# Last shared expert of a Perceiver layer: order of VectorE's sums, place of the routed answers, a GpSimd drain and the output in quarters

## The chip, the core and the metric

The kernel runs on one core of a Trainium2 chip. The metric is the device time of one execution in microseconds, the median of several runs. Three runs of the kernel before gave 1395.56, 1396.55 and 1399.64 us. All data is float32.

## What is computed

512 tokens (8 batches of 64, 512 wide) pass through three residual blocks. The first is cross-attention to 8 x 1601 context rows, with a rational weight in place of the exponential; the second is causal self-attention; the third, in which the change lies, is a mixture of experts:

```python
sh     = gelu(xf @ sW1 + sb1)             # two shared experts, every token
shared = mean over the two of (sh @ sW2 + sb2)
gates  = xf @ rW + rb                     # eight routed experts
probs  = softmax(top_k(gates, 2))         # two of them for each token
moe    = sum_j probs[:, j] * (gelu(xf @ W1[e_j] + b1[e_j]) @ W2[e_j] + b2[e_j])
x      = x + shared + moe
```

## The kernel before, in words

**Stages.** Attention fills the span to about 980 us and plays no part here. The expert stage then runs blocks one after the other in `run` (L1324): shared expert 0's last token tile, the first half of shared expert 1 (`Halves`, hidden quarters 0 and 1), eight routed experts (`Routed`, the fullest first, with gathered rows), and the second half of shared expert 1 (`Halves`, quarters 2 and 3, `store=True`). After that stands a loop (L1418) for tokens beyond the experts' room, whose trip count is read from a tensor; every engine reads the count and takes the branch.

**The token sum** `res` [128, 4, 512] lies in SBUF throughout: four token tiles (`tt`) of 128 rows. Everything is added to it in place, and at the end it is written to `out`.

**Halves.** Its matrix products are done in seven block products instead of eight (`ORDER`, L322). Each unit n adds one block product into a PSUM bank; three banks are used, A by units 0, 2, 4 and 6, C by unit 1, and B by units 3 and 5. Since a bank goes on collecting after it was read, a later unit of the same bank must wait until the earlier value has been read. There are three sections:

- `hidden(q)` (L1162) makes one hidden quarter in seven units of four matmuls. Units 0, 2 and 3 are copied from PSUM by ScalarE (L1191). Units 1, 4 and 5 are "joined" by VectorE, which adds PSUM to the copy (L1175), and then ScalarE applies gelu in two instructions (L1169). Unit 6 gets gelu straight from PSUM.
- `combine` (L1199) makes the four sums t1 to t4 (`RIGHT`) of each finished hidden quarter, which the seven products of the second layer need as operands. Each is a VectorE instruction with two SBUF inputs (L1210).
- `rows` (L1212) makes the second layer in seven units of eight matmuls (both quarters). VectorE adds each to `res` (L1231), halved, since two shared experts are averaged. Unit 2 is the first that reads a sum (t2).

**Routed answers.** Each routed expert writes its rows to `ys_d` in device memory. Two units into the last block (`at[NEXP + 2, 1]`), `combine(ys_d, from_i)` (L1378) runs on GpSimd: for every tile and each of the two picks an indirect DMA gathers the rows (L1383), a GpSimd instruction multiplies them by the probability (L1387), and another adds them to `res` (L1388). There are eight of each, and the buffers come from the pool `sd`, which has five.

**What sets the order.** The loops give instructions in program order, and a scheduler in the tile framework orders each engine's instructions by priority. In the program it made, VectorE's queue in the last block reads: three joins of quarter 2, its four sums, three joins of quarter 3, its four sums, then seven additions to `res`. PE, ScalarE and VectorE take their instructions strictly in this order. SP issues nearly all DMAs, also the four of the output (`rows_out`, L1103): tiles 2 and 3 after unit 5, tiles 0 and 1 after unit 6. GpSimd issues its own DMAs, the gathers among them. When the loop's branch is not taken, all engines meet in a closing barrier (L1486), in which each engine first executes a DRAIN.

Of the kernel before, what the change touches and what calls it, by code (L numbers as in the profile page):

```python
# [14 lines left out]
ALU = mybir.AluOpType  # L15
# [7 lines left out]
NTT = NT // P  # L23
# [5 lines left out]
NEXP, NSH = 8, 2  # L29
# [46 lines left out]
def perceiver_kernel(  # L76
# [7 lines left out]
    nc = tc.nc  # L84
# [22 lines left out]
    def w8(name):  # L107
        return w8p.tile([P, NC, 512], F32, tag="w8", name=name)

    def at4(name):  # L110
        return atp.tile([P, 1024], F32, tag="at", name=name)

    def np2(name):
        return npp.tile([P, 512], F32, tag="np", name=name)

    def sd(name):
        return sdp.tile([P, 512], F32, tag="sd", name=name)

    def psa(name):
        return ps_a.tile([P, 512], F32, tag="a", name=name)  # L120
# [49 lines left out]
    res = big.tile([P, NTT, E], F32, name="res")  # L170
# [31 lines left out]
    for j in range(2):  # L202
        m = mask[j * SQ : (j + 1) * SQ, 0, :]
        nc.gpsimd.affine_select(
            out=m, in_=m, compare_op=ALU.is_ge, fill=NEG, base=0,
# [10 lines left out]
        out=tri, in_=ones, compare_op=ALU.is_gt, fill=0.0, base=0,  # L216
# [12 lines left out]
    ys_d = dram.tile([TOT + 1, E], F32, name="ys_d")  # L229
# [76 lines left out]
    def right_parts(x):  # L306
        return {"b11": x[:, 0:2, 0:HF], "b12": x[:, 0:2, HF:SEC],
                "b21": x[:, 2:4, 0:HF], "b22": x[:, 2:4, HF:SEC]}

    RIGHT = (("t1", "b12", "b11"), ("t2", "b22", "t1"), ("t3", "b22", "b12"), ("t4", "b21", "t2"))  # L310
    tparts = {}

    def context_part(i, k):
        if k == 0:
# [7 lines left out]
    ORDER = (("A", "a11", "b11"), ("C", "a12", "b21"), ("A", "s2", "t2"), ("B", "s1", "t1"),  # L322
             ("A", "s3", "t3"), ("B", "s4", "b22"), ("A", "a22", "t4"))

    def multiply(ps, w, x, keys, first=True, last=True):

        for k in range(2):
            for c in range(2):
                l, r = (w, x) if keys else (x, w)

                nc.tensor.matmul(  # L331
                    ps[:, k, :], l[:, c, k * P : (k + 1) * P], r[:, c, :],
                    start=first and k == 0 and c == 0, stop=last and c == 1,
                    skip_group_check=True,
                )
# [78 lines left out]
    for c in range(NC):  # L414
        nc.gpsimd.dma_start(
            out=odd_x[:, c, :],
            in_=ctxT[:, c * P : (c + 1) * P, SKV - 1 : SKV].rearrange("b p s -> p (b s)"),
# [424 lines left out]
    for i, (b, k) in enumerate(secs):  # L842
        if i == 0:
            plan.add(4 * FULL, first_keys)
            there[i] = plan.now
            for t in range(SPT):
# [4 lines left out]
                if t == 1:  # L851
                    for g in range(NG):
                        plan.add(FULL, lambda g=g: q_unit(g))
                    asked = plan.now
# [54 lines left out]
    for tt in range(NTT):  # L909
        gap = 5.0 if tt < NTT - 1 else 3.2  # L910
        for bb in range(2):
            b = 2 * tt + bb
# [32 lines left out]
    pr = gp.tile([P, NTT, 2], F32, name="pr")  # L945
# [4 lines left out]
    from_i = gp.tile([P, 2, NTT], I32, name="from_i")  # L950
# [150 lines left out]
    outT = out.rearrange("(tt p) e -> tt p e", p=P)  # L1101

    def rows_out(tt):  # L1103
        nc.sync.dma_start(out=outT[tt], in_=res[:, tt, :])
# [38 lines left out]
    class Halves:  # L1143
# [18 lines left out]
        def hidden(self, q):  # L1162

            st = {}

            def gelu(f, r, src=None):
                for k in range(2):
                    hc = q * QC + 2 * f + k
                    nc.scalar.activation(  # L1169
                        st[f, r][:, k], (st[f, r] if src is None else src)[:, k], AF.Gelu,  # L1170
                        bias=b1_t[:, self.e, hc : hc + 1],
                    )

            def join(f, r, ps):
                nc.vector.tensor_tensor(st[f, r], ps, st[f, r], ALU.add)  # L1175
                gelu(f, r)

            def unit(n):
                bank, a, b = ORDER[n]
                if n == 0:  # L1180
                    self.h[q] = w8("hq")
                    for f in range(2):
                        for r in range(2):
                            st[f, r] = self.h[q][:, 2 * f : 2 * f + 2, r * HF : (r + 1) * HF]
                fresh = bank not in st
                if fresh:
                    st[bank] = psa("ps_hh").rearrange("p (k n) -> p k n", k=2)
                ps = st[bank]
                multiply(ps, self.w[0, q][a], self.x[b], True, first=fresh)
                if n in (0, 2, 3):  # L1190
                    nc.scalar.copy(st[{0: (0, 0), 2: (0, 1), 3: (1, 1)}[n]], ps)  # L1191
                elif n == 6:
                    gelu(1, 0, ps)
                else:
                    join(*{1: (0, 0), 4: (1, 1), 5: (0, 1)}[n], ps)

            return [lambda n=n: unit(n) for n in range(len(ORDER))]

        def combine(self):  # L1199

            k = len(self.right)
            for q in self.qs:
                p = self.right[q] = right_parts(self.h[q])
                t = at4("ht").rearrange("p (k c s) -> p k c s", k=2, c=2)
                if not k:
                    self.t4 = at4("ht").rearrange("p (k c s) -> p k c s", k=2, c=2)
                p |= {"t1": t[:, 0], "t2": t[:, 1], "t3": p["b12"], "t4": self.t4[:, k]}
                k += 1
                for d, a, b in RIGHT:
                    nc.vector.tensor_tensor(p[d], p[a], p[b], ALU.subtract)  # L1210

        def rows(self):  # L1212

            st = {}

            def unit(n):
                bank, a, b = ORDER[n]
                fresh = bank not in st
                if fresh:
                    st[bank] = psa("ps_hr").rearrange("p (k n) -> p k n", k=2)  # L1220
                ps = st[bank]
                if n == 0:
                    self.combine()
                for q in self.qs:
                    multiply(
                        ps, self.w[1, q][a], self.right[q][b], False,
                        first=fresh and q == self.qs[0], last=q == self.qs[-1],
                    )
                f, r = ((0, 0), (0, 0), (0, 1), (1, 1), (1, 1), (0, 1), (1, 0))[n]
                y = res[:, 2 * r : 2 * r + 2, f * 256 : (f + 1) * 256]  # L1230
                nc.vector.scalar_tensor_tensor(y, ps, 1.0 / NSH, y, ALU.mult, ALU.add)  # L1231
                if self.store and n >= 5:
                    for tt in ((2, 3), (0, 1))[n - 5]:
                        rows_out(tt)

            return [lambda n=n: unit(n) for n in range(len(ORDER))]

# [137 lines left out]
            skip_runtime_bounds_check_because="an index that max_index gave among eight",  # L1375
        )

    def combine(src, idx):  # L1378

        for tt in range(NTT):  # L1380
            for j in range(2):
                g = sd("g")
                nc.gpsimd.indirect_dma_start(  # L1383
                    out=g, out_offset=None, in_=src[:, :],
                    in_offset=bass.IndirectOffsetOnAxis(ap=idx[:, j, tt : tt + 1], axis=0),
                )
                nc.gpsimd.tensor_scalar_mul(g, g, pr[:, tt, j : j + 1])  # L1387
                nc.gpsimd.tensor_add(res[:, tt, :], res[:, tt, :], g)  # L1388

    tops = []  # L1390

    def routing():
        for tt in range(NTT - 1):
# [10 lines left out]
            (0, 3): routing,  # L1404
            (2, 2): lambda: probabilities(tops.pop()),
            (2, 6): add_biases,
            (NEXP + 2, 1): lambda: combine(ys_d, from_i),
        },
    )

# [7 lines left out]
    with tc.For_i(0, n_over) as j:  # L1418
        run([Routed(expert_in(ovx_i, j), TOT + j * P, P, yo_d, 0)])

        m = gp.tile([P, 2, NTT], F32, name="m_in")
        nc.vector.tensor_single_scalar(m, left, 0.0, op=ALU.is_ge)
        ix = gp.tile([P, 2, NTT], F32, name="ix")
        nc.vector.tensor_single_scalar(ix, left, float(P), op=ALU.is_lt)
        nc.vector.tensor_mul(m, m, ix)
        nc.vector.scalar_tensor_tensor(ix, left, float(-P), m, ALU.add, ALU.mult)
        nc.vector.tensor_scalar_add(ix, ix, float(P))
        ix_i = gp.tile([P, 2, NTT], I32, name="ix_i")
        nc.vector.tensor_copy(ix_i, ix)
        nc.vector.tensor_scalar_add(left, left, float(-P))  # L1430
        combine(yo_d, ix_i)
        for tt in range(NTT):
            rows_out(tt)
# [56 lines left out]
```

## Time and profile before

| what | value |
|---|---|
| median of three runs | 1396.55 us |
| the profiled execution's own time | 1398.13 us |
| its span, first to last instruction | 1396.3 us |
| outside the span | 1.8 us |
| mean granted TensorE clock | 0.995 |
| busy: PE, VectorE (DVE), ScalarE (ACT), GpSimd (POOL) | 1364.5, 890.0, 642.7, 770.7 us |
| last block: first matmul of its hidden part | 1330.9 us |
| second layer (`ps_hr`): first matmul | 1360.6 us |
| last addition to `res` begins | 1384.95 us |

How to read it. A line of the timeline has the start in us, the length in us (of merged instructions, the whole stretch), the engine, the line of the kernel, the operation, what it writes and reads with sizes, and how many were merged. The bracket says how long the engine was idle before and whose end released it. "PE" are matmuls and "PEld" weight loads; a float32 matmul makes two records. A q behind an engine's name (SPq, POOLq) marks its instruction queue, with instructions that only wait, branch, drain or issue. The table of windows gives busy times in chosen stretches and the granted TensorE clock (PEclk, 1.00 is full).

### The profile page before, as it was taken

To read this page: it belongs to the slowest core of one execution; us is meant where nothing else is said; L and a number is where in the kernel's file an instruction comes from. 1 tells how busy PE (TensorE), PEld (TensorE's weight loads), DVE (VectorE), ACT (ScalarE), POOL (GpSimd) and SP (SyncE) were. 2 spreads that over 40 slices of the span, in tenths; PEclk is the share of its full clock that TensorE was granted. 3 is DMA by queue.
4 is the path that set the end of the run, shared out by engine and by line. 5 is a ranking of instruction groups with operands and counts; after the bars stand their busy time and mean duration, and the time that the engine had idled before them with its cause. 6 is when DMAs were issued, how large, how long until landed. Compare 5 with 4: busy or idle time off the path is not lost.

```text
span 1396.3 us, 36461 instructions
## 1 busy us (share of the span) xinstructions
PE 1364.5 (98%) x16080; PEld 1075.3 (77%) x16080; DVE 890.0 (64%) x646; ACT 642.7 (46%) x1339; POOL 770.7 (55%) x688
## 2 busy tenths in 40 slices
PE   8999999999999999999999999999999999999996
PEld 3678788787788787788878777555786799977775
DVE  4698999988899997889989988614420000000332
ACT  3556666566666666566656666322311111112230
POOL 6388899886789986878887877500200000000063
PEclk9999999999999999999999999999999999999998
DMA  7002112112400121111121115354555346789621
GB/s 228 31 3 70 32 33 77 62 33 70 160 32 32 47 92 40 32 64 39 47 92 33 62 49 187 97 191 159 193 208 199 126 176 239 280 319 325 219 61 38
DMA packets 84227, 156.34 MB, mean 112 GB/s; under 512 B 13306, under 2 KB 13338, under 8 KB 84068
## 3 DMA queue, kind: packets, MB, share of 16 engines
q1 hardware_dynamic: 77732, 136.94, 28.5%
q0 software_dynamic: 4704, 13.91, 2.9%
q10 hardware_dynamic: 1632, 3.15, 0.7%
q8 instruction: 127, 2.08, 0.6%
q14 instruction: 32, 0.26, 0.1%
HBM read 143.24 MB, written 10.72 MB: 110 GB/s over the span
## 4 chain that ended last, share of the span: by engine, by line
PE 86%; DVE 4%; ACT 4%; POOL 2%; issue 2%; DMA 0%; DVEq 0%; POOLq 0%
PE ps_k L331 17%; PE ps_v L331 16%; PE ps_h L1351 11%; PE y L1296 6%; PE ps_s L520 4%; PE y L1305 4%; PE ps_hr L331 3%; PE ps_o L570 3%; PE ps_h L817 3%; PE y L829 3%; PE ps_hh L331 3%; DVE neg L538 3%; PE ps_v L399 1%; PE ps_k L389 1%; ACT neg L535 1%
## 5 line engine op out<-in xcount | busy, mean ns | idle before, releaser
L538 DVE RECIPROCAL neg<-neg 128x512 f32<-128x512 f32 (+1 forms) x224 | 683.8, 3092 | 58.4 <-ACT neg L537 55.2
L539 POOL TENSOR_TENSOR at<-at,neg 128x512 f32<-128x512 f32 (+1 forms) x224 | 266.6, 1196 | 126.7 <-DVE neg L538 122.7
L551 POOL TENSOR_TENSOR tot<-tot,at 128x512 f32<-128x512 f32 (+1 forms) x176 | 223.9, 1272 | 12.8
L1351 PEld LDWEIGHTS ps_h<-xgT,w1t 128*128 128x128 f32 x1024 | 147.9, 191 | 38.5 <-issue 32.7
L1356 ACT ACTIVATE hT<-ps_h,b1e 128x128 f32<-128x128 f32 (+4 forms) x128 | 50.3, 393 | 261.0 <-PE ps_h L1351 235.0
L1287 POOL DMA_DIRECT2D ys_d<-yo x12 | 6.6, 549 | 287.2 <-DVE yo L1286 287.2
L537 ACT ACTIVATE neg<-neg,one_t 128x512 f32<-128x512 f32 (+1 forms) x224 | 162.2, 726 | 0.0
L1351 PE MATMUL ps_h<-xgT,w1t 128*128 128x128 f32 (+4 forms) x1024 | 161.0, 301 | 0.0
L535 ACT ACTIVATE neg<-ps_s 128x512 f32<-128x512 f32 (+1 forms) x224 | 130.2, 583 | 63.2 <-PE ps_s L520 51.8
L331 PE MATMUL ps_k<-tx,sk 128*128 128x256 f32 x552 | 129.8, 386 | 3.8 <-ACT kT L348 3.7
L536 ACT ACTIVATE at<-ps_s 128x512 f32<-128x512 f32 (+1 forms) x224 | 131.7, 591 | 0.0
L331 PE MATMUL ps_v<-sv,tx 128*128 128x256 f32 x552 | 129.0, 384 | 1.0 <-ACT v L344 1.0
L331 PEld LDWEIGHTS ps_k<-tx,sk 128*128 128x128 f32 x552 | 101.5, 190 | 23.5 <-ACT kT L348 4.5
L331 PEld LDWEIGHTS ps_v<-sv,tx 128*128 128x128 f32 x552 | 102.4, 190 | 17.2 <-ACT v L344 1.4
L1278 DVE COPY xgT<-pt_x 128x512 f32<-128x512 f32 (+3 forms) x12 | 6.8, 592 | 142.7 <-PE pt_x L1277 142.7
L1296 PE MATMUL y<-w2t,hT 128*128 128x512 f32 x192 | 96.1, 595 | 0.0
L344 ACT COPY v<-ps_v 128x512 f32<-128x512 f32 x92 | 56.0, 609 | 75.0 <-PE ps_v L331 75.0
L348 ACT ACTIVATE kT<-ps_k,bk_t 128x256 f32<-128x256 f32 x138 | 59.6, 499 | 60.0 <-PE ps_k L331 60.0
L331 PE MATMUL ps_k<-cx,wk 128*128 128x256 f32 x368 | 86.9, 385 | 0.0
L331 PE MATMUL ps_v<-wv,cx 128*128 128x256 f32 x368 | 86.1, 383 | 0.0
L520 PEld LDWEIGHTS ps_s<-qT,kT 32*64 32x64 f32 x6144 | 70.1, 130 | 18.6 <-issue 17.2
L331 PEld LDWEIGHTS ps_k<-cx,wk 128*128 128x128 f32 x368 | 68.1, 190 | 12.9 <-issue 2.3
(264 smaller groups left out, 2042.2 us busy)
## 6 DMA issues: line engine op xcount, KB each, us to landing
w1t<-in_W_dram SPq DMA_DIRECT2D x32, 1024.0 KB, 11.6
w2t<-in_W_dram SPq DMA_DIRECT2D x32, 1024.0 KB, 12.2
cx<-in_ctxT_dram SPq DMA_DIRECT2D x23, 1024.0 KB, 5.8
w1t<-in_sW_dram SPq DMA_DIRECT2D x12, 1024.0 KB, 5.1
w2t<-in_sW_dram SPq DMA_DIRECT2D x12, 1024.0 KB, 5.4
wo<-in_woT_dram SPq DMA_DIRECT2D x4, 1024.0 KB, 5.3
awq<-in_aWq_dram SPq DMA_DIRECT2D x4, 1024.0 KB, 5.2
awp<-in_aWp_dram SPq DMA_DIRECT2D x4, 1024.0 KB, 5.4
```

The source lines that it names most:

```text
L331: nc.tensor.matmul(ps[:, k, :], l[:, c, k * P : (k + 1) * P], r[:, c, :], start=first and k == 0 and c == 0, stop=last and c == 1, skip_gr ...
L344: nc.scalar.copy(dst, src)
L348: nc.scalar.activation(dst[:, k], src[:, k], AF.Identity, bias=bk_t[:, g : g + 1])
L520: nc.tensor.matmul(ps[j][h, k, g, :], kT[rows, g, h], qT[rows, g, b * SQ : (b + 1) * SQ], start=True, stop=True, skip_group_check=True,)
L535: nc.scalar.activation(neg, ps, AF.Relu, scale=-1.0)
L536: nc.scalar.activation(pos, ps, AF.Relu)
L537: nc.scalar.activation(neg, neg, AF.Identity, bias=one_t[:w])
L538: nc.vector.reciprocal(neg, neg)
L539: nc.gpsimd.tensor_add(pos, pos, neg)
L551: nc.gpsimd.tensor_add(tot, tot, at[:, :, i])
L1296: nc.tensor.matmul(self.y[k], hT[:, s : s + w], w2t, start=first, stop=last)
L1351: nc.tensor.matmul(ph[:, : blk.n], w1t[:, c, f : f + P], blk.x[:, c, :], start=c == 0, stop=c == NC - 1,)
```

## The change

- **Sums behind joins.** `combine` makes the sums of both quarters together, tied behind the last join (`issue_after(self.joined.ins)`), t1 and t2 of both first, then t3 and t4. VectorE's queue in both `Halves` blocks is now: six joins, eight sums, then the additions.
- **VectorE joins the routed answers.** GpSimd's multiply and add are dropped. After each of the additions of units 0 to 3 in the last block, VectorE executes two `scalar_tensor_tensor` on 128x512 (gathered rows times probability plus `res`, all from SBUF): the two answers of one tile.
- **GpSimd only gathers, and is drained.** All eight gathers are issued together, into buffers that come alternately from the pools `np` and `sd`. A `drain` on GpSimd stands directly behind the eighth.
- **Rows leave in quarters by two queues.** After units 3, 4, 5 and 6 a quarter of `res` (two tiles, 256 columns) is written, one tile by SP, one by ScalarE's queue: four DMAs of 128 KB on each in place of four of 256 KB on SP. The last unit's addition is made as two instructions of 128x256, one for each tile.

The overflow loop uses the same gather and join, and keeps whole-tile writes.

```diff
@@ Halves.hidden
             def join(f, r, ps):
-                nc.vector.tensor_tensor(st[f, r], ps, st[f, r], ALU.add)
+                self.joined = nc.vector.tensor_tensor(st[f, r], ps, st[f, r], ALU.add)
                 gelu(f, r)
@@ Halves.combine
-            for q in self.qs:
+            for k, q in enumerate(self.qs):
                 p = self.right[q] = right_parts(self.h[q])
...
-                for d, a, b in RIGHT:
-                    nc.vector.tensor_tensor(p[d], p[a], p[b], ALU.subtract)
+            with tc.issue_after(self.joined.ins):
+                for part in (RIGHT[:2], RIGHT[2:]):
+                    for q in self.qs:
+                        p = self.right[q]
+                        for d, a, b in part:
+                            nc.vector.tensor_tensor(p[d], p[a], p[b], ALU.subtract)
@@ Halves.rows
-                nc.vector.scalar_tensor_tensor(y, ps, 1.0 / NSH, y, ALU.mult, ALU.add)
-                if self.store and n >= 5:
-                    for tt in ((2, 3), (0, 1))[n - 5]:
-                        rows_out(tt)
+                for k in ((0, 1) if self.store and n == len(ORDER) - 1 else (slice(0, 2),)):
+                    added = nc.vector.scalar_tensor_tensor(
+                        y[:, k], ps[:, k], 1.0 / NSH, y[:, k], ALU.mult, ALU.add
+                    )
+                if not self.store:
+                    return
+                if n < NTT:
+                    with tc.issue_after(added.ins):
+                        for j in range(2):
+                            join_answer(back.pop((n, j)), n, j)
+                for f, r, at_n in ((0, 0, 3), (1, 1, 4), (0, 1, 5), (1, 0, 6)):
+                    if n == at_n:
+                        for k, queue in enumerate((nc.sync, nc.scalar)):
+                            tt = 2 * r + k
+                            fs = slice(f * 256, (f + 1) * 256)
+                            queue.dma_start(out=outT[tt, :, fs], in_=res[:, tt, fs])
@@ the routed answers
-                g = sd("g")
-                nc.gpsimd.indirect_dma_start(
...
-                nc.gpsimd.tensor_scalar_mul(g, g, pr[:, tt, j : j + 1])
-                nc.gpsimd.tensor_add(res[:, tt, :], res[:, tt, :], g)
+    def gather(src, idx, tt, j):
+        g = sd("g") if j else np2("g")
+        asked = nc.gpsimd.indirect_dma_start(
...
+        return g, asked
+    def join_answer(g, tt, j):
+        nc.vector.scalar_tensor_tensor(
+            res[:, tt, :], g, pr[:, tt, j : j + 1], res[:, tt, :], ALU.mult, ALU.add
+        )
+    def gather_all():
+        for tt in range(NTT):
+            for j in range(2):
+                back[tt, j], asked = gather(ys_d, from_i, tt, j)
+        with tc.issue_after(asked.ins):
+            nc.gpsimd.drain()
...
-            (NEXP + 2, 1): lambda: combine(ys_d, from_i),
+            (NEXP + 2, 1): gather_all,
```

More of the change, by code (lines that the diff above doesn't have):

```diff
@@ L1199, in combine @@
         def combine(self):
-            k = len(self.right)
-            for q in self.qs:
+            self.t4 = at4("ht").rearrange("p (k c s) -> p k c s", k=2, c=2)
+            for k, q in enumerate(self.qs):
                 p = self.right[q] = right_parts(self.h[q])
                 t = at4("ht").rearrange("p (k c s) -> p k c s", k=2, c=2)
-                if not k:
-                    self.t4 = at4("ht").rearrange("p (k c s) -> p k c s", k=2, c=2)
                 p |= {"t1": t[:, 0], "t2": t[:, 1], "t3": p["b12"], "t4": self.t4[:, k]}
-                k += 1
-                for d, a, b in RIGHT:
-                    nc.vector.tensor_tensor(p[d], p[a], p[b], ALU.subtract)
+            with tc.issue_after(self.joined.ins):
[4 more added lines that the diff above has]
+                            nc.vector.tensor_tensor(p[d], p[a], p[b], ALU.subtract)
         def rows(self):
@@ L1376, in expert_in @@
         )
+    def gather(src, idx, tt, j):
+        g = sd("g") if j else np2("g")
+        asked = nc.gpsimd.indirect_dma_start(
+            out=g, out_offset=None, in_=src[:, :],
+            in_offset=bass.IndirectOffsetOnAxis(ap=idx[:, j, tt : tt + 1], axis=0),
+        )
[3 more added lines that the diff above has]
+            res[:, tt, :], g, pr[:, tt, j : j + 1], res[:, tt, :], ALU.mult, ALU.add
+        )
+    back = {}
+    def gather_all():
[4 more added lines that the diff above has]
+            nc.gpsimd.drain()
     def combine(src, idx):
@@ L1381, in combine @@
             for j in range(2):
-                g = sd("g")
-                nc.gpsimd.indirect_dma_start(
-                    out=g, out_offset=None, in_=src[:, :],
-                    in_offset=bass.IndirectOffsetOnAxis(ap=idx[:, j, tt : tt + 1], axis=0),
-                )
-                nc.gpsimd.tensor_scalar_mul(g, g, pr[:, tt, j : j + 1])
-                nc.gpsimd.tensor_add(res[:, tt, :], res[:, tt, :], g)
+                join_answer(gather(src, idx, tt, j)[0], tt, j)
     tops = []
```

## The prediction

> **What bounds the kernel now.** First the chain of work that ended last: by engine it is matmul, and each part of the change must be a gap in it or its end.
>
> ```profile
> PE 86%; DVE 4%; ACT 4%; POOL 2%; issue 2%; DMA 0%; DVEq 0%; POOLq 0%
> ```
>
> Then PE's timeline of the last block, for a matmul that waited:
>
> ```profile
> 1347.31 3.62 PE L331 MATMUL ps_hh<-xt,sw 128*128 128x256 f32 x16
> 1353.61 2.82 PE L331 MATMUL ps_hh<-xt,sw 128*128 128x256 f32 x8 [2.68 <-ACT hq L1191]
> 1356.22 2.79 PE L331 MATMUL ps_hh<-xnT,sw 128*128 128x256 f32 x8
> 1358.85 1.89 PE L331 MATMUL ps_hh<-xt,w1t 128*128 128x256 f32 x8
> ```
>
> This is PE's only wait on another engine in the last block. Unit 4 of the last hidden quarter adds into the bank that ScalarE must first have copied for unit 2. After the wait eight records take 2.8 us, where they take 1.89. ScalarE and VectorE tell why:
>
> ```profile
> 1352.18 0.91 ACT L1169 ACTIVATE hq<-hq,b_t 128x256 f32<-128x256 f32 x2 [5.81 <-DVE hq L1175]
> 1352.99 1.05 ACT L1191 COPY hq<-ps_hh 128x512 f32<-128x512 f32 x2
> ...
> 1343.99 0.97 DVE L1210 TENSOR_TENSOR ht<-hq 128x512 f32<-128x512 f32 x1 [0.97 <-ACT hq L1169]
> 1345.00 3.19 DVE L1210 TENSOR_TENSOR ht<-hq,ht 128x512 f32<-128x512 f32 x1
> 1348.11 1.76 DVE L1210 TENSOR_TENSOR hq<-hq 128x512 f32<-128x512 f32 x1
> 1349.79 1.75 DVE L1210 TENSOR_TENSOR ht<-hq,ht 128x512 f32<-128x512 f32 x1
> 1351.46 0.68 DVE L1175 TENSOR_TENSOR hq<-ps_hh,hq 128x512 f32<-128x512 f32 x1
> ```
>
> The copy stands on ScalarE behind a gelu that waits 5.81 us for the join, and the join stands on VectorE behind four sums, which take 7.67 us where four of 0.69 would take 2.8. At the same time GpSimd executes multiplies and adds (from 1342.80 to 1354.20).
>
> Windows give the clock, and the list of the closing line gives the end:
>
> ```profile
> 1350.90:1353.60 2.70, 0.03 (x1) 0.00 (x0) 1.24 (x2) 1.42 (x4) 2.70 (x3) 1.00 0.00 0
> 1353.60:1358.00 4.40, 4.39 (x13) 3.58 (x14) 0.69 (x1) 1.18 (x3) 3.90 (x4) 0.62 0.22 60
> ...
> L1486 POOLq DRAIN  x3: 46/109/5140, 1390.3 to 1396.0; - x3
> L1486 SPq DRAIN  x3: 7/7/7, 1391.0 to 1395.7; - x3
> ...
> L1104 SPq DMA_DIRECT2D out_dram<-res x4: 332/370/1486, 1382.3 to 1386.1; - x4
> ```
>
> PE stands still and then gets a clock of 0.62. At the end GpSimd's first closing DRAIN takes 5.14 us from 1390.3, though its last add ended at 1372.2; the next takes 0.11.
>
> **1. Sums behind the joins.** In order of VectorE's queue the join of unit 1 no longer has sums ahead of it. In the three other hidden quarters, where no stretched sums stood ahead, PE never waited. At full clock sixteen records start every 3.45 us (1343.86 to 1347.31), so unit 4 would have started at 1350.76, not 1353.61: 2.85 us. The sixteen records from 1353.61 to 1358.85 took 5.24 in place of 3.45: 1.79. Together 4.6 us of PE, all on the path. The Trainium skill (TensorE: Matmul & The Clock Gate, section What's actually happening) has the half clock follow an idle window of about 3.4 us; by it a wait of 2.85 should cost nothing more, and this part would be worth 2.9. The row shows 0.62 right behind this wait and 1.00 two windows later, so I take 4.6. Ends: 2.9 and 4.7.
>
> What is late next? Eight sums now lie behind the last join, in both Halves blocks. Undisturbed they take 8 x 0.69 = 5.5 us. The last join ends 0.8 us before the second layer starts (1359.74 against 1360.58), so they end 4.7 after its start. Behind them stands the addition of unit 0, whose bank unit 2 needs 6.9 us after the start (two units of 3.45): with 0.69 the addition ends at 5.4, 1.5 us to spare. t2 of both quarters is ready by about 3.3. In the first Halves block the same holds (join ends 1017.55, rows start 1018.38), and no PE wait was there to win: nothing. GpSimd issues three DMAs there from 1018.55 to 1020.25 beside two-input sums, which stay at 0.69.
>
> **2. Answers on VectorE, gathers alone on GpSimd.** Removed: eight GpSimd multiplies of 1.59 and eight adds of 1.28, none on the chain. Added: eight VectorE instructions of 128x512. None is in the trace from SBUF with two inputs and a multiply; the nearest row is the addition at L1231, 0.69; even as long as the worst sum's mean here (7.67/4 = 1.92) they would sum to 15.4. I take 8 x 0.69 = 5.5. With sums, answers and additions VectorE works 5.5 + 5.5 + 4.8 = 15.8 us beside 24.2 us of PE: hidden. If the cover went, at most 1.5 us at the first bank. Behind a waiting answer would stand the additions that free PE's banks. The gathers were issued at 1337.91 and every 1.31 after, landing after 3.7 (median); their buffers are free (the new pool's were read by matmuls that end by 1333.7). Eight so end at 1337.91 + 8 x 1.31 + 3.7 = 1352.1; the first answer is due about 5.4 after the second layer's new start (1360.6 - 4.6 = 1356.0), 1361.4. No wait: nothing.
>
> **3. The drain.** In the changed program's order it stands directly behind the eighth gather, so 1348.4 to about 1353.5, with nothing behind it on GpSimd but reading the loop count, needed 20 us later. What it costs there lies beside PE; a loss is excluded for that reason. What it saves is open between 0 (the price is that of the closing, or of the 1.43 us semaphore instruction that still comes between) and: the barrier releases after the last engine, which would be SP, whose second DRAIN begins 1391.07. GpSimd went on at 1395.50. Saved: 4.4 us. A rule speaks against: the Trainium skill (VectorE: DVE Perf Modes, section The DRAIN you can't avoid) calls closing DRAINs a constant of some 12 ns on all engines, by which moving it is worth nothing. SP's row agrees (7 ns); GpSimd's does not (5140). Since it has idled 18 us before, the 5.14 is not waiting for unfinished work but work of the drain, done once: the two drains behind it take 0.11 and 0.05. I take 4.4.
>
> **4. Quarters by two queues.** Now: from the start of the last addition (1384.95) 0.72 to the first issue, 0.38 to the second, which took 1.49 where others take 0.37, and landing 2.2 us later (median to landing): SP's wait ended at 1389.33, 4.38 after. Then: two additions of 0.42 (row of 128x256 PSUM additions, L697: 0.42), the second DMA issued on ScalarE's idle queue at 0.87, landing at most 2.2 later: 3.1, a gain of 1.3. If the slow issue recurs on ScalarE (1.12 more) the gain is 0.2; with half the bytes up to 1.6. I take 1.0. The eight DMAs hold back nothing: behind them on SP and ScalarE stands only the count's reading (0.3 and 0.5 us), done while the last one lands. The barrier's own steps are as before.
>
> **Sum.** 4.6 + 4.4 + 1.0 = 10.0 us. The profiled execution took 1398.13 (span 1396.3 and 1.8 around it), which becomes 1388.1; it lies 1.6 above the median. For the median: 1396.55 - 10.0 = 1386.5.
>
> **Rivals.**
>
> A: the closing drain keeps its price. For it: the row names no cause, and a semaphore instruction of 1.43 us still runs between. Against: 18 us of idleness, and the short second drain. 1396.55 - 4.6 - 1.0 = 1390.9.
>
> B, slower: VectorE's two-input work stays stretched, now in front of the banks. Place: eight sums, then the addition of unit 0. At 1.92 each they take 15.4, and the addition ends 15.3 after the start instead of 6.9: PE waits 8.4, with 1.8 of half clock. Four answers at 1.92 and three additions before unit 4 (0.7 each, as before) make that one late by some 2, with 1.8 again: 14.0 lost, 1396.6 - 10.0 + 14.0 = 1400.6. It decides from 10 us on. For it: the stretched rows above. Against: they stretch only beside GpSimd's multiplies and adds, which are gone; the drain ends 2.5 us before the second layer starts; and the sums at 1018.52 stayed at 0.69 beside GpSimd's DMA issues. To lose, GpSimd would have to hold VectorE until 15 us into the second layer.
>
> C: part 1 fails, since another wait takes its place at unit 4 or 2, with drain and quarters kept: 1396.55 - 5.4 = 1391.2.
>
> **How the numbers follow.** Forecast 0.72 (1385.0 to 1388.5 by the ends of parts 1 and 4), A 0.19, C 0.06, B 0.03. A measurement can tell about 0.3% (4.2 us) from no change, so the bound is 1392.4. Faster: 0.72 + 0.18 of A + 0.02 of C = 0.92; the rest of A and C is within, 0.05; slower 0.03. The range reaches from 1384.8 over A and C to 1391.8; outside are B and their tails.
>
> **What would show it.** Right: PE's timeline from 1331 to its end without a wait on ScalarE and with clock 1.00; sums at 0.6 to 0.7; four DRAINs on GpSimd with the 5 us one at about 1348 and a short one at the end; last addition near 1380.3, span near 1386.3. Wrong: a PE wait at unit 2 or 4 of the second layer (B), a closing DRAIN near 5 us (A), or an issue over 1 us on ScalarE's queue (part 4).

## The result and the profile after

The changed kernel takes 1387.21 us (median of six runs, 1385.32 to 1387.64), the kernel before 1397.08 (six runs beside them, 1395.56 to 1399.64). The ratio is 0.9924, with a 95% interval from 0.9912 to 0.9937: 9.9 us faster, where 10.0 were forecast (the forecast median, 1386.5, counted from the three runs of before, 1396.55).

The profiled execution took 1385.32 us, span 1383.6; the one of before 1396.3. Marks that both traces have divide these 12.7 us:

| stretch | before | after | difference |
|---|---|---|---|
| start to the last block's first weight load | 1330.48 | 1327.98 | -2.5 |
| its hidden part, to the second layer's first weight load | 29.88 | 25.24 | -4.64 |
| second layer, to the start of the last addition | 24.59 | 24.59 | 0 |
| from there to the end | 11.33 | 5.82 | -5.51 |

The first line is not the change's (the last section traces it); its gain in the profile is the other two, 10.2. PE's timeline of the last block after:

```profile
1344.80 5.34 PE L331 MATMUL ps_hh<-xt,sw 128*128 128x256 f32 x24
1349.98 1.89 PE L331 MATMUL ps_hh<-xnT,sw 128*128 128x256 f32 x8
1351.71 1.89 PE L331 MATMUL ps_hh<-xt,w1t 128*128 128x256 f32 x8
1353.44 7.07 PE L331 MATMUL ps_hr<-w2t,hq 128*128 128x256 f32 x32
```

No bracket is left: the wait on ScalarE's copy is gone, and eight records take 1.89. ScalarE and VectorE, in this order:

```profile
1345.79 0.91 ACT L1169 ACTIVATE hq<-hq,b_t 128x256 f32<-128x256 f32 x2 [1.92 <-DVE hq L1175]
1346.73 0.59 ACT L1191 COPY hq<-ps_hh 128x512 f32<-128x512 f32 x1
```

```profile
1345.06 0.69 DVE L1175 TENSOR_TENSOR hq<-ps_hh,hq 128x512 f32<-128x512 f32 x1 [4.54 <-PE ps_hh L331]
...
1352.52 0.68 DVE L1212 TENSOR_TENSOR ht<-hq 128x512 f32<-128x512 f32 x1
1353.23 0.69 DVE L1212 TENSOR_TENSOR ht<-hq,ht 128x512 f32<-128x512 f32 x1
...
1357.46 0.68 DVE L1235 SCALAR_TENSOR_TENSOR res<-ps_hr,res 128x512 f32<-128x512 f32 x1
1358.17 1.54 DVE L1405 SCALAR_TENSOR_TENSOR res<-g,pr,res 128x512 f32<-128x512 f32 x2
...
1377.81 0.76 DVE L1235 SCALAR_TENSOR_TENSOR res<-ps_hr,res 128x256 f32<-128x256 f32 x2 [2.76 <-PE ps_hr L331]
```

The join at 1345.06 had only PE to wait for; ScalarE's gelu waited 1.92 us for it, where it had waited 5.81. The sums take under 0.7 each and stand behind the last join. Two answers of a tile take 1.54. Last the instructions of GpSimd's new drain and of the closing line:

```profile
L1417 POOLq DRAIN  x1: 12047/12047/12047, 1338.4 to 1338.4; - x1
```

```profile
L1520 POOLq DRAIN  x3: 34/49/109, 1382.0 to 1383.4; - x3
L1520 SPq DRAIN  x3: 7/7/7, 1382.8 to 1383.1; - x3
```

The drain's row begins while gathers still stand in GpSimd's own work; the last of those ends at 1345.28, and the drain 5.2 us later, at 1350.5. Of the closing drains none is over 0.11 us.

### The profile page after: what moved, and what is told of

Its sections match the earlier page's. It is cut to its first block, busy times and chain, and to the rows that moved or that the text cites. A ratio compares the mean times of both kernels' runs of the same rounds, so it can differ in the third digit from the quotient of the medians.

```text
span 1383.6 us, 36463 instructions
## 1 busy us (share of the span) xinstructions
PE 1360.6 (98%) x16080; PEld 1073.2 (78%) x16080; DVE 888.9 (64%) x655; ACT 642.8 (46%) x1339; POOL 745.5 (54%) x672
## 3 DMA queue, kind: packets, MB, share of 16 engines
q0 software_dynamic: 4704, 13.91, 2.9%
## 4 chain that ended last, share of the span: by engine, by line
PE 87%; ACT 4%; DVE 4%; POOL 3%; issue 2%; DMA 0%; DVEq 0%; POOLq 0%
PE ps_k L331 17%; PE ps_v L331 16%; PE ps_h L1367 11%; PE y L1312 6%; PE ps_s L520 4%; PE y L1321 4%; PE ps_hr L331 3%; PE ps_hh L331 3%; PE ps_o L570 3%; PE ps_h L817 3%; PE y L829 3%; DVE neg L538 3%; PE ps_v L399 1%; ACT neg L535 1%; PE ps_k L389 1%
```

## The experiments

Two questions were open: which part does what it was credited with, and what the drain's 5 us are. The theory at the start was the prediction's: the place of the sums ends PE's wait, the drain is work that can be done earlier, the quarters give about 1 us. Each experiment ran in five rounds or more beside the kernel before, whose median in these sets was 1397.0 to 1397.5; ratios are to it.

**1. The changed kernel with its sums back between the joins.**

```diff
-            with tc.issue_after(self.joined.ins):
-                for part in (RIGHT[:2], RIGHT[2:]):
-                    for q in self.qs:
...
+                for d, a, b in RIGHT:
+                    nc.vector.tensor_tensor(p[d], p[a], p[b], ALU.subtract)
```

> The changed kernel with one part undone: the four sums of a hidden quarter stand between the joins again, as before; answers on VectorE, drain and quarters stay. Theory S (stretch): the stall of 2.9 us and its half clock of 1.8 came from GpSimd's multiplies and adds stretching the sums from 2.8 to 7.7 us. With these gone the sums take 0.6 to 0.7 each, the join of unit 1 is in time, and PE does not wait: 1387.2, equal to the changed kernel. Rival P (place): the sums ahead of the join are what makes it late, stretched or not: PE waits before unit 4 of the last hidden quarter and the time rises by up to 4.6, to 1391.8.

Measured: 1387.9 us (1385.89 to 1389.97), ratio 0.9931 [0.9915, 0.9947]. VectorE's timeline:

```profile
1343.64 0.69 DVE L1175 TENSOR_TENSOR hq<-ps_hh,hq 128x512 f32<-128x512 f32 x1 [0.96 <-PE ps_hh L331]
1345.30 0.69 DVE L1210 TENSOR_TENSOR ht<-hq 128x512 f32<-128x512 f32 x1 [0.97 <-ACT hq L1169]
1346.03 0.69 DVE L1210 TENSOR_TENSOR ht<-hq,ht 128x512 f32<-128x512 f32 x1
1346.64 0.69 DVE L1210 TENSOR_TENSOR hq<-hq 128x512 f32<-128x512 f32 x1
1347.24 0.68 DVE L1210 TENSOR_TENSOR ht<-hq,ht 128x512 f32<-128x512 f32 x1
1349.22 0.69 DVE L1175 TENSOR_TENSOR hq<-ps_hh,hq 128x512 f32<-128x512 f32 x1 [1.30 <-issue]
```

The four sums stand ahead of a join, as before the change. But they take 2.6 us and not 7.67, and end 1.3 us before that join begins. PE doesn't wait, and the hidden part takes 25.24 us as in the changed kernel. So without GpSimd's multiplies and adds the place of the sums is worth nothing that these runs can resolve.

**2. The kernel before with its sums behind the joins, and nothing else** (the first two hunks of the change).

> The kernel before with one part done: sums of both quarters behind the last join; GpSimd still multiplies and adds, no drain of its own, rows leave as before. Theory S: the stall at unit 4 of the last hidden quarter goes (4.6 won), but the eight sums meet GpSimd's multiplies and adds, take about 1.9 each, and unit 2 of the second layer waits for the addition of unit 0 by up to 8 us, with 1.8 of half clock: between 1397 and 1402. Rival P: the place alone wins the stall, 1392.5.

Measured: 1394.56 us (21 runs), ratio 0.998 [0.9973, 0.9986]. Neither number was met. The stall at unit 4 is gone (hidden part 25.24), so the place alone cures it too. The sums hardly stretch now, one pair of them to 1.78: from 1355.9 to 1361.5, where they stand, GpSimd mostly issues gathers and executes one multiply (1358.86). That they fell into this gap was not foreseen, and is luck of the order. But PE's timeline has a new wait, in the second layer:

```profile
1363.76 7.07 PE L331 MATMUL ps_hr<-sw,ht 128*128 128x256 f32 x32
1372.32 7.17 PE L331 MATMUL ps_hr<-sw,hq 128*128 128x256 f32 x32 [1.49 <-DVE res L1233]
```

VectorE's timeline tells whose it is:

```profile
1363.96 0.69 DVE L1233 SCALAR_TENSOR_TENSOR res<-ps_hr,res 128x512 f32<-128x512 f32 x1 [1.81 <-PE ps_hr L331]
1371.57 1.29 DVE L1233 SCALAR_TENSOR_TENSOR res<-ps_hr,res 128x512 f32<-128x512 f32 x2 [6.92 <-POOL res L1390]
```

An addition to `res` waits 6.9 us for GpSimd's routed answer to the same tile, and PE for the bank behind it. GpSimd's answers end at 1371.5 here, no later than before (1372.2), but the second layer starts 3.7 us earlier (1356.85, before 1360.58). The second layer takes 26.35 in place of 24.59. Of 4.6 us won, 1.8 are given back; the median's 3.0 us agree with the 2.8 that are left.

**3. The changed kernel without its drain** (the two lines with `drain` left out).

> The changed kernel without the drain behind the gathers. Theory D: the drain's price is paid once at the first drain after gathers, wherever it stands; GpSimd's closing drain takes 5.1 us again, and the time rises by 4.4 to 1391.6. Rival: the closing drain was long in the kernel before because of the multiplies and adds on GpSimd, which are gone anyway; the closing drain is then under 0.3 us and the time stays at 1387.2.

Measured: 1391.6 us (1390.49 to 1392.16), ratio 0.9956 [0.9942, 0.9969]; 4.4 more than the changed kernel. The closing line:

```profile
L1518 POOLq DRAIN  x3: 46/109/5136, 1383.9 to 1389.6; - x3
L1518 SPq DRAIN  x3: 7/7/7, 1384.7 to 1389.3; - x3
```

**4. The kernel before with a drain behind GpSimd's last add, and nothing else.**

```diff
-                nc.gpsimd.tensor_add(res[:, tt, :], res[:, tt, :], g)
+                added = nc.gpsimd.tensor_add(res[:, tt, :], res[:, tt, :], g)
+        if src is ys_d:
+            with tc.issue_after(added.ins):
+                nc.gpsimd.drain()
```

> The kernel before with one part done: a drain on GpSimd behind its last add of a routed answer. Theory D: it runs from 1372.2 for 5.2 us, beside PE, and the closing drain is short: 1397.1 - 4.4 = 1392.7. Rival: the 5.1 us belong to the closing itself or to the semaphore instruction of 1.43 us ahead of it: 1397.1, no change.

Measured: 1393.67 us (7 runs), ratio 0.9973 [0.996, 0.9987]; 3.9 less than before.

```profile
L1391 POOLq DRAIN  x1: 6473/6473/6473, 1369.9 to 1369.9; - x1
```

It ends at 1376.3, 5.2 us after the last add; the longest closing drain is 0.11. Added alone or taken away, the drain is worth what it was forecast to be, within the intervals.

**5. The changed kernel with whole-tile writes on SP**, after units 5 and 6 as before, and the last addition in one instruction.

```diff
-                for f, r, at_n in ((0, 0, 3), (1, 1, 4), (0, 1, 5), (1, 0, 6)):
...
+                if n >= 5:
+                    for tt in ((2, 3), (0, 1))[n - 5]:
+                        rows_out(tt)
```

> The changed kernel with its output as before: whole tiles of 256 KB, all from SP, after units 5 and 6, and the last addition in one instruction. Theory Q: the quarters and the second queue shorten the stretch from the start of the last addition to the end of the span, which is 5.8 us in the changed kernel, by 1.1; it becomes 6.9, and the time 1388.3. Rival: the last transfer's fixed part is all of it and the queues don't matter: 5.8, and 1387.2.

Measured: 1387.75 us (1387.35 to 1391.79), ratio 0.9932 [0.9919, 0.9945]. From the last addition to the end the profile has 7.16 us, and the changed kernel's 5.82. Issues and landings of the output:

```profile
L1104 SPq DMA_DIRECT2D out_dram<-res x4: 333/391/1722, 1380.0 to 1383.9; - x4
...
DMA to landing us min/median/max: 2.0/2.3/3.3
```

The changed kernel's:

```profile
L1250 SPq DMA_DIRECT2D out_dram<-res x4: 332/344/357, 1361.3 to 1378.3; - x4
...
L1250 ACTq DMA_DIRECT2D out_dram<-res x4: 338/366/383, 1362.8 to 1378.6; - x4
...
DMA to landing us min/median/max: 1.7/2.1/2.8
```

The slow issue is back with the whole tiles, 1.72 us. But the 1.34 between the two ends is not all the edit's: in every trace a transfer of 16 KB that is marked as instructions (an instruction fetch) begins 1.13 to 1.15 us after the last addition's start (1.51 in experiment 9). It took 1.31 us here and 0.99 in the changed kernel's profile. Quartered kernels whose fetch took 1.31 (experiments 7 and 8) end after 6.2 us; against these the whole tiles cost 1.0. The medians, 0.5 us apart, do not resolve it.

The fetch bears on both forms. With quarters the last issue begins at 0.79 us, before it; in the changed kernel 240 of the last 256 packets of 1 KB have ended by 2.18 us, and 16, one DMA engine's share, follow one another to 3.09, 0.95 after the fetch. With whole tiles the second issue begins beside the fetch, and in all four such traces it ends 0.37 us after the fetch does; an ordinary issue takes about as long. In us after the last addition's start:

| run | second issue begins | fetch ends | second issue ends |
|---|---|---|---|
| before | 1.10 | 2.22 | 2.59 |
| experiment 2 | 1.10 | 2.58 | 2.95 |
| experiment 4 | 1.10 | 2.59 | 2.96 |
| experiment 5 | 1.10 | 2.45 | 2.83 |

So the slow issue goes with the fetch. That the fetch causes it is not shown; nor do these runs separate the size of the tiles from the time of the issue, since the edit puts back both the whole tiles and the undivided addition.

**6. The changed kernel with all eight quarters on SP** (`enumerate((nc.sync, nc.sync))`).

> The changed kernel with the quarters, but all eight transfers from SP. Theory Q: the second queue only saves the 0.4 us of one issue, and that beside the second half of the last addition; the stretch from the last addition to the end is 5.8 to 6.1 us, the time 1387.2 to 1387.5, so the quarters' size makes the gain. Rival: the second queue makes it: the stretch is about 6.9 us as with whole tiles, 1388.3.

Measured: 1389.08 us (1386.54 to 1391.25), ratio 0.9938 [0.9925, 0.995]. SP's wait for the landing ends 4.12 us after the last addition's start with a fetch of 1.43; by two queues it was 4.08 with a fetch of 1.39 (experiment 1). SP's last issue begins at 0.88 us here, still ahead of the fetch, and takes 0.38. So the earlier landing comes from the quarters with their divided addition, not from the second queue, which is worth at most 0.4 us in the steps of the barrier. The rest of the median's 1.9 us is not explained: this profile has a PE wait of 0.61 behind a late join, which the edit doesn't touch. In the profiles of experiments 5 (1.06) and 7 (0.43) PE stands still at this place too, and in the changed kernel's it doesn't; why is open.

**7 and 8. Where the drain's 5 us come from.** In both, the changed kernel's drain is moved on GpSimd: ahead of all eight gathers, behind the last write to `ys_d` (`wrote[0]`), as the diff shows, or ahead of the last gather alone (seven gathers, the drain, one gather).

```diff
-        with tc.issue_after(asked.ins):
-            nc.gpsimd.drain()
+        with tc.issue_after(wrote[0].ins):
+            dr = nc.gpsimd.drain()
+        with tc.issue_after(dr.ins):
+            for tt in range(NTT):
+                for j in range(2):
+                    back[tt, j], asked = gather(ys_d, from_i, tt, j)
```

> The changed kernel with its drain moved ahead of the eight gathers, behind the last routed expert's write. Theory U: the drain's price is paid anew whenever gathers or other GpSimd DMAs came since the last drain; the closing drain takes 5.1 us again, 1391.6. Rival O: the price is paid once in a program, at its first drain after the start; the closing drain is short, 1387.2. Rival N: the price goes by the number of GpSimd DMAs since the last drain (8 of some 65): the closing drain is between 0.5 and 1.5 us, and hidden behind SP's own closing steps, 1387.2 to 1388.

> The changed kernel with its drain ahead of the last of the eight gathers. Theory U: one gather behind the drain is enough, the closing drain takes 5.1 us, 1391.6. Rival N: the price goes by the number, so that one gather costs under 0.7 us, hidden behind SP's closing steps: 1387.2.

Measured: 1388.63 us (1388.34 to 1390.28), ratio 0.9936 [0.9923, 0.9949], and 1387.44 us (1386.41 to 1389.68), ratio 0.993 [0.9917, 0.9943]. Drains of experiment 7, then 8:

```profile
L1417 POOLq DRAIN  x1: 5054/5054/5054, 1336.2 to 1336.2; - x1
```

```profile
L1524 POOLq DRAIN  x3: 46/109/705, 1387.1 to 1388.4; - x3
L1524 SPq DRAIN  x3: 7/7/7, 1387.8 to 1388.1; - x3
```

```profile
L1521 POOLq DRAIN  x3: 46/109/133, 1385.9 to 1387.2; - x3
```

The longest closing drain is 0.705 with eight gathers behind the moved drain, 0.133 with one, and the last closing drain, behind no DMA, 0.046. That is (0.705 - 0.046) / 8 = 0.082 and 0.087 us for each DMA. The kernel has 62 DMAs issued by GpSimd (the groups' counts summed), and 5.14 / 62 = 0.083. In experiment 7, 54 of them lie ahead of the drain: 54 x 0.083 = 4.48, and the row without the 0.56 in which the last write is still being issued is 4.49. So a drain is charged for every DMA that GpSimd has issued since the last drain. By bytes (2.1 of 13.9 MB) the eight gathers would have had 0.77 us and by packets (640 of 4704) 0.70, where 0.66 were measured and 8 x 0.083 is 0.66. One drain is off the line: the moved one of experiment 8, with 61 DMAs ahead, ends 5.37 us after the seventh gather, where 62 took 5.15 to 5.30 in the other profiles. That a drain is cheap because the engine has just been drained, or dear because something is unfinished, is excluded: 18 idle us didn't lower it, and eight gathers that had long landed raised it. The 0.705 costs nothing here, since SP's drain begins 0.7 to 0.8 after GpSimd's in both kernels.

**9 and 10. The half clock at 1070 us** (see the last section). In 9 the bias products of the mixture are made on 128 rows, filled with zeros, and not on 10; in 10 they are made one at a time, behind every second unit of the first routed expert.

```diff
+        nc.vector.memset(b2_t, 0.0)
...
+        nc.vector.memset(wT, 0.0)
...
-            nc.tensor.matmul(ps, wT[:NE, tt, :], b2_t[:NE], start=True, stop=True)
+            nc.tensor.matmul(ps, wT[:, tt, :], b2_t, start=True, stop=True)
```

```diff
             (2, 6): add_biases,
+            **{(2, 7 + 2 * tt): lambda tt=tt: add_bias(tt) for tt in range(NTT)},
```

> The changed kernel, with the four bias products of the mixture made on all 128 rows (both operands filled up with zeros) in place of the 10 that carry data; the result is the same sum. Nearly every profiled execution so far shows one or two windows of half clock of 3.4 us each between 1069 and 1076 us, directly behind these four products (eight records, 3.7 us, without idle on PE), each worth some 1.7 us. Theory W (the clock is granted by the work that PE's rows do, and 10 rows in 128 count as hardly any): full rows leave the clock at 1.00 there, span 1.7 to 3.4 below the others with such windows, median about 1384.5 where the changed kernel has 1387.2. Rival (the clock falls there for another reason: the transposes, the weight loads, or nothing in this place): the windows stay, median 1387.2 to 1388.

> The changed kernel, with the four bias products no longer one behind the other: one behind every second unit of the first routed expert (0.9 us each, with 7 us of ordinary products between). Theory W: no stretch of several us is left in which PE's rows are mostly empty, so the half-clock windows at 1069 to 1076 us go, median about 1384.5. Theory W in a weaker form (what counts is a fixed window's mean, and 0.9 of 3.4 us is enough) keeps some of them: 1386. Rival (another cause): the windows stay, 1387.2 to 1388.

Measured: 1385.95 us (1385.28 to 1388.7), ratio 0.992 [0.9906, 0.9933], and 1387.04 us (1386.74 to 1388.07), ratio 0.9927 [0.9913, 0.9942]. Neither profile has a half-clock window at this place. The lower median of the first is 1.3 us under the changed kernel's; their intervals overlap, so it isn't shown to be faster, only to be no slower. In 10 the spreading costs something itself: from the weights' transposes (L1093) to the last block the profile has 264.1 us, and the changed kernel's, without a window too, 263.0.

## Why the prediction was right, and where it was not

**1, sums behind the joins, 4.6 us.** The size is right (29.88 to 25.24 is 4.64), its owner is not. The stall needed two things: sums ahead of the join, and GpSimd's multiplies and adds beside them, which stretched them from 2.6 to 7.67 us. The change removes both, and either alone ends the stall (experiments 1 and 2). The step "In order of VectorE's queue the join of unit 1 no longer has sums ahead of it" is true and would be enough, but the whole 4.6 was booked on it and "nothing" on part 2, though the prediction itself had written that the sums stretch only beside GpSimd's work. The half clock behind the wait went with it: 1.8 of the 4.6, as the row had said, though an idle stretch of 2.7 us is shorter than the window of some 3.4 in the Trainium skill (TensorE: Matmul & The Clock Gate, section What's actually happening); here the measurement decides.

**2, answers on VectorE, 0.** Two answers take 1.54 us, so 0.77 each for the 0.69 that was taken. They are hidden. The addition of unit 0 ended 4.7 us after the second layer's start; it had 6.9. Rival B did not come: the sums were not stretched. But this part is not worth nothing. Without part 1 it also ends the stall (experiment 1), and it is what keeps PE from the wait of experiment 2, where GpSimd's answers came too late for a layer that starts 4.6 us sooner. "What is late next?" was asked for part 1 within the whole change only.

**3, the drain, 4.4 us.** Right: 4.4 when taken away, 3.9 when added alone. It ended at 1350.5, not 1353.5, since the gathers began earlier and came every 1.26. The reason "work of the drain, done once" was right for the time but too coarse: the work is 0.083 us for each DMA since the last drain. Rival A fell. Of the rule that closing DRAINs are a constant of some 12 ns on all engines (the Trainium skill, VectorE: DVE Perf Modes, section The DRAIN you can't avoid) SP's 7 ns remain; GpSimd's 5136 ns in experiment 3 contradict it.

**4, quarters by two queues, 1.0 us.** SP's wait for the landing ended 0.8 earlier (3.58 after the last addition's start, 4.38 before), and the closing steps gave about 0.3. At an equal instruction fetch the profile has 1.0, but no median resolves it, so this term rests on profiles. The landing was taken at 3.1 and came at 3.58: the sum had no term for the instruction fetch, behind which one engine's share of the last rows came late. The slow issue did not recur; the prediction read its 1.49 without a cause, and in the traces it ends with the fetch. The second queue was credited with what the quarters do on SP alone (experiment 6).

**Sum.** 4.6 + 4.4 + 1.0 = 10.0 forecast, 9.9 in the medians. The terms add up because they lie behind one another on the path. The total doesn't depend on whether part 1 or part 2 is credited with the 4.6, so that it came out is no proof of the split.

## What to carry to other kernels

When a wait needs two conditions, price each part of a change with the other part absent as well; otherwise the first part gets credit that the second would have earned alone, and the wait that comes next goes unseen. An engine that stands idle at the end of a kernel can still hold the closing barrier: count the DMAs that GpSimd issued and drain it behind the last, where other engines still have work. At the end of a kernel look for the instruction fetch too: it took between 0.89 and 1.61 us here, so a gain of 1 us there is hardly more than it moves the end from run to run.

## What the runs showed of the hardware

**GpSimd's drain** cost 0.083 us for each DMA that it had issued since the last one: 5.14 for 62, 4.49 for 54, 0.66 for 8, 0.09 for 1. The 5.37 for 61 of experiment 8 are 0.3 over it.

**Half clock behind a wait.** PE waits of 2.68 us (before) and 2.66 (experiment 4) were followed by a window of 3.41 us at half clock; those of 1.49 (experiment 2), 1.06, 0.61 and 0.43 were not.

**Half clock without an idle PE.** In nine of the ten profiles with the bias products as they were (the changed kernel's is the tenth), one or two windows of 3.41 us at half clock lie between 1068 and 1077 us. The kernel before, PE's timeline:

```profile
1067.21 3.70 PE L1098 MATMUL ps_b<-b_t,wT 10*128 10x512 f32 x8
1070.84 3.34 PE L1351 MATMUL ps_h<-xgT,w1t 128*128 128x256 f32 x8
```

and experiment 9, with the same products on all rows:

```profile
1069.69 3.70 PE L1100 MATMUL ps_b<-b_t,wT 128*128 128x512 f32 x8
1073.23 1.89 PE L1369 MATMUL ps_h<-xgT,w1t 128*128 128x256 f32 x8
```

Eight ordinary records behind the products of 10 rows took 3.34 us, and 1.89 behind the full ones. Each window costs about 1.7 us. PE's matmul records have no gap there, so that the products were thin, not absent, seems to be what counts; two profiles without a window, of kernels that differ in these products alone, speak for it and are few. Such a window is 1.7 of the 2.5 us by which the two profiles differ ahead of the last block. The other 0.8 arise earlier, ahead of the first half of shared expert 1, which begins at 992.92 us before and at 992.11 after and takes the same time in both.
